# Two graph layers on one core: hand-written places for the first and last pairs, first loads through two queues, the last pair's products plain

## The chip, the cores and the metric

The kernel runs on one core of one Trainium2 chip. The metric is the device time of one execution in microseconds (us); the median of three runs is given. TensorE (PE) multiplies matrices into PSUM; its weight loads are shown as PEld. VectorE (DVE), ScalarE (ACT) and GpSimd (POOL) do the elementwise work, and SyncE (SP) and ACT issue the transfers here. Each engine works through its own list of instructions in order.

## The reference

x holds 128 graphs of 128 nodes with 512 features, float32; one 128 x 128 adjacency matrix is shared by all. Layer 0 is attention with 8 heads of 64 features, masked by the adjacency, added to x and normalised. Layer 1 is a graph attention layer whose edge scores come from two vectors, added to its input and normalised.

```python
def _L0_gnn_ref(x, adj, Wq, bq, Wk, bk, Wv, bv, Wo, bo):
    q = (x @ Wq + bq).reshape(b, n, H, HD)      # k and v alike
    scores = jnp.einsum('bqhd,bkhd->bhqk', q, k) / jnp.sqrt(jnp.float32(HD))
    scores = scores + (1.0 - adj)[None, None, :, :] * -1000000000.0
    attn = jax.nn.softmax(scores, axis=-1)
    out = jnp.einsum('bhqk,bkhd->bqhd', attn, v).reshape(b, n, d)
    return out @ Wo + bo

def _L1_gnn_ref(x, W, a, beta, mask):
    h = jnp.einsum('bnc,cf->bnf', x, W)
    s1 = jnp.einsum('bnf,f->bn', h, a1); s2 = jnp.einsum('bnf,f->bn', h, a2)
    e = jax.nn.leaky_relu(s1[:, :, None] + s2[:, None, :], negative_slope=ALPHA) * mask[None]
    att = jax.nn.softmax(e, axis=2)
    h_prime = jnp.einsum('bij,bjf->bif', att, h)
    return jax.nn.elu(h_prime + beta * h)

x = _layernorm(x + _L0_gnn_ref(x, adj, ...), axis=-1)
x = _layernorm(x + _L1_gnn_ref(x, ..., adj), axis=-1)
```

## The kernel before

**Pairs.** The 128 graphs are worked on in 64 pairs (`G = 2`, `NG = 64`); b0 and b1 are the two batches of pair g. Everything is float32.

**Products by seven.** The five matrix products of a pair (q, k, v with Wq, Wk, Wv; w with Wo; h with layer 1's W) are each split in two along the rows of the weight, along its columns and along the two batches, and made from 7 block products in place of 8 (a Strassen-Winograd scheme). The weight's sums and differences are made once (`weight_sums`, L183 to L192; one of the four operations, L189, overwrites a block of the weight itself), those of x, of the attention output oT and of the aggregated zT for each pair on POOL (`block_sum`, L222). `product(name, g, n)` issues block product n (8 matmuls of 128 columns in the trace's count for q and k, L265, 4 of 256 columns for v, w and h, L259) and accumulates in PSUM; `take_part`, `take_block` and `add_block` read the intermediate sums out, on ACT (L275, L279) and DVE (L289, L311, L319). Between two products that add into the same place a part must have been read.

**A pair's way.** `fetch_blocks` loads x in blocks of 32 and `turn_x` (L202) transposes them on DVE. q and k products, `scores` (L333), `mask` and `row_max` on DVE, `exps` and `normalise` on ACT (L355, L369). The attention weights are written to DRAM (`attn_write`, L376), read back in another arrangement (`attn_read`, L381), and turned on DVE (`turn_attn`, L398). `attend` (L408) multiplies with v, `attend_evict` (L418) gives oT, the w products add the residual x, then comes the norm: `bn_stats`, `bn_aggr`, `add_eps`, `inv_std` (a power on POOL, L441). `row_product` and `scale_s` give the edge vectors, `spread_s2` (L473) spreads one over the partitions, `edge`, `leaky`, `edge_max`, `edge_exp`, `weights` make the edge softmax for both batches, `turn_weights` (L513) and `weights_evict` transpose it, `aggregate` (L527) applies it, the h products follow, then `elu_max`, `elu_exp`, `elu_sum`, a second norm, `norm_f` (L555) and `store` (L561). The tile u that is stored has two buffers.

**Order.** Each step is put in one list by `at(place, fn, ...)`. `lay(g)` gives the steps of pair g the place `g * STEP` plus a number written by hand, the same numbers for every pair (L577 to L657). The list is sorted by place and the instructions are issued in that order (L671), so an engine's list is what the places make it. A pair's steps reach from -34.63 to 136.33 with `STEP = 37.33`: four to five pairs are under way at once.

**The start.** Before the list, SP issues the x blocks of pair 0, then wq and wk by halves of the columns in turn, wv, x of both batches, wo and w1 (L116 to L138). wq, wk and wv are loaded "turned": four transfers, each to 32 partitions (`load_turned`). ACT issues the small ones: biases, adjacency, and four broadcasts over the partitions. The two constants made from the adjacency and beta are made at once on DVE (L147, L149). `wa_column` (L158) on DVE, `wa_turn` (L168) on TensorE and `wa_centre` on DVE make the two rows of layer 1's edge vectors from w1.

**Buffers.** PSUM is one pool of eight banks for everything (`ps_mm`). The small statistics are in `st` with three buffers.

Of the kernel before, what the change touches and what calls it, by code (L numbers as in the profile page):

```python
# [22 lines left out]
def gnn_two_layers(  # L23
# [49 lines left out]
    st = ctx.enter_context(tc.tile_pool(name="st", bufs=3))  # L73
# [3 lines left out]

    def load_blocks(g):
        t = grp.tile([P, G, 4, P], F32, tag="xb", name=f"xblk_{g}", bufs=1)
        for a in range(4):  # L80
            nc.sync.dma_start(
                out=t[a * Q : (a + 1) * Q].rearrange("r t b d -> r (t b) d"),
                in_=x[g * G : (g + 1) * G, :, a * P : (a + 1) * P].rearrange(
                    "t (b r) d -> r (t b) d", r=Q
                ),
            )
        return t
# [10 lines left out]
    def load_turned(t, src, cols):  # L98
        for a in range(4):
            nc.sync.dma_start(  # L100
                out=t[a * Q : (a + 1) * Q, :, cols],
                in_=src[a * P : (a + 1) * P, cols].rearrange("(m c) f -> c m f", c=Q),
            )
# [12 lines left out]
    xblk = {0: load_blocks(0)}  # L116
    for half in range(2):
        cols = slice(half * HF, (half + 1) * HF)
        load_turned(wq_sb, wq, cols)
        load_turned(wk_sb, wk, cols)  # L120
        if half == 0:
            bq_c = column(bq, "bq_c")
            bk_c = column(bk, "bk_c")
    load_turned(wv_sb, wv, slice(0, D))
    adj_sb = cpool.tile([P, N], F32, tag="adj_sb", name="adj_sb")
    nc.scalar.dma_start(out=adj_sb, in_=adj)
    xn = {b: load_x(b) for b in range(G)}
    bo_b = broadcast(cpool, bo, D, "bo_b")
# [5 lines left out]
    ]  # L134
    wo_sb = cpool.tile([P, NC, D], F32, tag="wo_sb", name="wo_sb")
    nc.sync.dma_start(out=wo_sb, in_=wo.rearrange("(c p) f -> p c f", p=P))
    w1_sb = cpool.tile([P, NC, D], F32, tag="w1_sb", name="w1_sb")
    nc.sync.dma_start(out=w1_sb, in_=w1.rearrange("(c p) f -> p c f", p=P))  # L138
# [3 lines left out]
    make_identity(nc, ident)  # L142
    mhalf = cpool.tile([P, G], F32, tag="mhalf", name="mhalf")
# [3 lines left out]
    nc.vector.tensor_scalar(amask, adj_sb, 1.0, NEG, ALU.subtract, ALU.mult)  # L147

    beta_i = cpool.tile([P, P], F32, tag="beta_i", name="beta_i")  # L149
    nc.vector.tensor_scalar(beta_i, ident, beta_b, None, ALU.mult)  # L150
# [32 lines left out]
    def weight_sums(name, w_sb, eng):  # L183
        t = cpool.tile([P, 3, G, HF], F32, tag=f"s_{name}", name=f"s_{name}")
        a11, a21 = w_sb[:, :2, :HF], w_sb[:, :2, HF:]
        a12, a22 = w_sb[:, 2:, :HF], w_sb[:, 2:, HF:]
        s2, s3, s4 = t[:, 0], t[:, 1], t[:, 2]
        eng.tensor_tensor(s3, a11, a21, ALU.subtract)
        eng.tensor_tensor(a21, a21, a22, ALU.add)  # L189
        eng.tensor_tensor(s2, a21, a11, ALU.subtract)  # L190
        eng.tensor_tensor(s4, a12, s2, ALU.subtract)
        left[name] = {1: a11, 2: a12, 3: s4, 4: a22, 5: a21, 6: s2, 7: s3}  # L192
# [47 lines left out]
    def product(name, g, n):  # L240
# [15 lines left out]
        a, b = left[name][n], first_blocks(name if name in "wh" else "x", g)[n]  # L256
# [37 lines left out]
    def block(name, g, i, j):  # L294

        if name in "qk":
            return OUT[name][g][:, 2 * i : 2 * i + 2, j * N : (j + 1) * N]
        return OUT[name][g * G + j][:, i * HF : (i + 1) * HF]

    def result(name, g):  # L300
        if name in "qk":
            OUT[name][g] = grp.tile([P, NC, G * N], F32, tag=name, name=f"{name}T_{g}", bufs=1)
        else:
            for b in range(g * G, (g + 1) * G):
                OUT[name][b] = wk2.tile([P, D], F32, tag=name, name=f"{name}_{b}")
# [86 lines left out]
    attnT, po, x1, stats, mv, ve, rstd, s12 = ({} for _ in range(8))  # L392
# [42 lines left out]
    def add_eps(g, name):  # L435
        ve[name, g] = st.tile([P, G], F32, tag=f"ve{name}", name=f"ve_{name}_{g}")
        nc.vector.tensor_scalar(ve[name, g], mv[name, g][:, :, 1], EPS, None, ALU.add)  # L437

    def inv_std(g, name):
        rstd[name, g] = st.tile([P, G], F32, tag=f"rstd{name}", name=f"rstd_{name}_{g}")  # L440
        nc.gpsimd.tensor_tensor(rstd[name, g], ve.pop((name, g)), mhalf, ALU.pow)  # L441
# [10 lines left out]
    def scale_s(g):  # L452
        s = st.tile([P, G, 2], F32, tag="s12n", name=f"s12n_{g}")
        r = rstd["c", g].rearrange("p (i o) -> p i o", o=1).broadcast_to([P, G, 2])
        nc.vector.tensor_tensor(s, s12[g], r, ALU.mult)
        s12[g] = s

    def norm_c(b):
# [3 lines left out]
            x1[b], y.pop(b), mv["c", g][:, i, 0:1], rstd["c", g][:, i : i + 1],  # L462
# [6 lines left out]
    def spread_s2(g):  # L469

        pb[g] = ps_mm.tile([P, G, N], F32, tag="mm", name=f"pb_{g}")
        for i in range(G):
            nc.tensor.transpose(pb[g][:, i, :], s12[g][:, i, 1:2].broadcast_to([P, P]), ident)  # L473

    def edge(g, i):

        if i == 0:
            ev[g] = wk2.tile([P, G, N], F32, tag="ev", name=f"ev_{g}", bufs=1)
        nc.vector.scalar_tensor_tensor(
            ev[g][:, i, :], pb[g][:, i, :], s12[g][:, i, 0:1], adj_sb, ALU.add, ALU.mult  # L480
        )

    def leaky(g):
        ee[g] = wk2.tile([P, G, N], F32, tag="ee", name=f"ee_{g}", bufs=1)
        nc.vector.scalar_tensor_tensor(ee[g], ev[g], ALPHA, ev[g], ALU.mult, ALU.max)

    def edge_max(g):
        emax[g] = st.tile([P, G], F32, tag="emax", name=f"emax_{g}")
        nc.vector.tensor_reduce(emax[g], ee[g], AX.X, ALU.max, negate=True)

    def edge_exp(g):
        esum[g] = st.tile([P, G], F32, tag="esum", name=f"esum_{g}")
        for i in range(G):
            nc.scalar.activation(
                ee[g][:, i, :], ee[g][:, i, :], AF.Exp, bias=emax[g][:, i : i + 1],
                accum_out=esum[g][:, i : i + 1],
            )

    def edge_inv(g):
        einv[g] = st.tile([P, G], F32, tag="einv", name=f"einv_{g}")  # L500
        nc.vector.reciprocal(einv[g], esum.pop(g))

    def weights(g, i):
        if i == 0:
            att[g] = wk2.tile([P, G, N], F32, tag="att", name=f"att_{g}", bufs=1)
        nc.vector.scalar_tensor_tensor(
            att[g][:, i, :], ee[g][:, i, :], einv[g][:, i : i + 1], beta_i, ALU.mult, ALU.add
        )

    def turn_weights(g):  # L510
        pat[g] = ps_mm.tile([P, G, N], F32, tag="mm", name=f"pat_{g}")
        for i in range(G):
            nc.tensor.transpose(pat[g][:, i, :], att[g][:, i, :], ident)  # L513

    def weights_evict(g):
        attT[g] = wk2.tile([P, G, N], F32, tag="attT", name=f"attT_{g}", bufs=1)
        nc.scalar.copy(attT[g], pat.pop(g))  # L517
# [19 lines left out]
    def elu_exp(b):  # L537
        nc.scalar.activation(hp[b], hp[b], AF.Exp)  # L538

    def elu_max(b):  # L540
        u[b] = wk2.tile([P, D], F32, tag="uf", name=f"u_{b}")
        nc.vector.scalar_tensor_tensor(u[b], hp[b], 0.0, x1.pop(b), ALU.max, ALU.add)  # L542
# [4 lines left out]
    def shift(g):  # L547
        nmr[g] = st.tile([P, G], F32, tag="nmr", name=f"nmr_{g}")
        nc.vector.scalar_tensor_tensor(
            nmr[g], mv["f", g][:, :, 0], -1.0, rstd["f", g], ALU.mult, ALU.mult  # L550
# [16 lines left out]
    def fetch_x(b):  # L567
        if b not in xn:
            xn[b] = load_x(b)
# [7 lines left out]
    def lay(g):  # L577
        t0 = g * STEP
        b0, b1 = g * G, g * G + 1

        def put(*rows):
            for place, fn, *args in rows:
                at(t0 + place, fn, *args)

        put(
# [7 lines left out]
            (-9.82, take_part, "q", g, 6, 1, 0), (-9.42, result, "k", g),  # L593
            (-9.42, add_block, "k", g, 0, 0, 2, 1), (-9.15, product, "q", g, 7),
            (-8.93, take_part, "k", g, 6, 1, 0), (-8.00, product, "k", g, 7),
            (-7.11, product, "q", g, 5), (-6.81, fetch_x, b0), (-6.21, product, "k", g, 5),
            (-6.00, take_part, "q", g, 5, 1, 1), (-5.62, result, "q", g),
# [11 lines left out]
            (9.49, exps, b0, 3), (9.53, result, "v", g), (9.53, add_block, "v", g, 0, 0, 2, 1),  # L609
            (10.50, row_inv, b0), (10.92, normalise, b0, 0), (11.50, product, "v", g, 6),  # L610
            (11.52, normalise, b0, 1), (12.37, product, "v", g, 7),
            (12.59, take_part, "v", g, 6, 1, 0), (12.97, normalise, b0, 2),
            (13.57, normalise, b0, 3), (14.17, exps, b1, 0), (14.39, attn_write, b0),
            (14.96, exps, b1, 1), (16.45, exps, b1, 2), (16.72, product, "v", g, 5),
            (17.24, exps, b1, 3), (17.39, attn_read, b0), (18.03, take_part, "v", g, 5, 1, 1),
            (18.25, row_inv, b1), (18.67, normalise, b1, 0), (19.27, normalise, b1, 1),
            (19.52, add_block, "v", g, 1, 1, 7, 5), (20.25, normalise, b1, 2),
            (20.85, normalise, b1, 3), (21.67, attn_write, b1), (24.67, attn_read, b1),
# [86 lines left out]
```

## Time and profile before

| | us |
|---|---|
| three runs | 2444.12, 2446.80, 2444.03 |
| median | 2444.12 |
| the profiled execution: its time | 2446.15 |
| the profiled execution: its span, first to last instruction | 2444.3 |
| mean granted clock of TensorE | 0.992 |
| HBM read, written | 140.32 MB, 100.66 MB |

The profile is of one execution. Busy time says how long an engine worked, with its share of the span; a wait is put down to the event that came last before the engine went on. "Granted clock" is the share of full speed that TensorE's throttle allowed. In the time line a row gives the start, the length, the engine, the line and the operation, what it writes and reads, the count, and in brackets the idle time before it and what ended that.

### The profile page before, as it was taken

How to read it: one execution, taken by the hardware profiler on the slowest of the kernel's cores; microseconds unless marked ns; L12 is line 12 of the kernel's file. 1: busy time of each engine (PE TensorE's matmuls, PEld its weight loads, DVE VectorE, ACT ScalarE, POOL GpSimd, SP SyncE). 2: the span in 40 equal slices, each digit the busy share in tenths (PEclk: the TensorE clock that was granted, in tenths of full speed). 3: DMA queues.
4: the chain of work that ended last, by engine and by line, in shares of the span. 5: the costliest groups of instructions: out<-in, count | busy, mean ns of one | idle time of the engine just before them, and what ended most of it. 6: DMA issues, size and time to landing. Idle time of an engine off the chain costs nothing. (4 is left out here: it accounts for less than half of the span.)

```text
span 2444.3 us, 50024 instructions
## 1 busy us (share of the span) xinstructions
PE 2387.3 (98%) x17928; PEld 2210.7 (90%) x17928; DVE 1916.2 (78%) x4386; ACT 1489.5 (61%) x5313; POOL 859.8 (35%) x1043
## 2 busy tenths in 40 slices
PE   6999999999999999999999999999999999999995
PEld 5899999999999999999999999999999999999984
DVE  5687787787787877877877877877877878778775
ACT  3556656656656656666566566566566566666662
POOL 4233324324323333333333333243243233333331
PEclk9999999999999999999999999999999999999997
DMA  6234234234233243343343342342342432433421
GB/s 178 78 87 121 86 97 122 79 104 119 79 106 111 81 113 101 83 121 96 87 121 91 91 122 84 99 121 79 105 118 73 113 107 79 118 99 84 122 87 35
DMA packets 205144, 244.25 MB, mean 100 GB/s; under 512 B 20576, under 2 KB 153824, under 8 KB 204896
## 3 DMA queue, kind: packets, MB, share of 16 engines
q1 hardware_dynamic: 202592, 240.20, 34.2%
q8 instruction: 142, 2.33, 0.4%
q10 hardware_dynamic: 2304, 0.86, 0.2%
q14 instruction: 106, 0.87, 0.1%
HBM read 140.32 MB, written 100.66 MB: 99 GB/s over the span
## 5 line engine op out<-in xcount | busy, mean ns | idle before, releaser
L355 ACT ACTIVATE s<-s,nmax 128x128 f32<-128x128 f32 x1024 | 397.7, 394 | 0.0
L369 ACT ACTIVATE sb<-s,rinv 128x128 f32<-128x128 f32 x1024 | 327.0, 392 | 25.6 <-DVE rinv L362 24.6
L222 POOL TENSOR_TENSOR tw<-oT 128x256 f32<-128x256 f32 x64 | 46.4, 725 | 793.3 <-DVE oT L418 793.3
L389 POOL TENSOR_TENSOR x<-x,bo_b_in 128x512 f32<-128x512 f32 x128 | 163.8, 1291 | 386.3 <-DMA x<-in_x_dram 385.6
L279 ACT ACTIVATE part_q<-pq,bq_c 128x128 f32<-128x128 f32 x384 | 118.7, 360 | 259.8 <-PE pq L265 259.8
L355 ACT ACTIVATION_READ_ACCUMULATOR s<-s,nmax 128x1 f32 x1024 | 196.5, 192 | 0.0
L279 ACT ACTIVATE part_k<-pk,bk_c 128x128 f32<-128x128 f32 x384 | 119.9, 363 | 114.5 <-PE pk L265 60.7
L517 ACT COPY attT<-pat 128x256 f32<-128x256 f32 x64 | 23.8, 372 | 272.2 <-PE pat L513 272.2
L341 DVE SCALAR_TENSOR_TENSOR s<-psc,amask 128x512 f32<-128x512 f32 x256 | 164.3, 684 | 27.1 <-PE psc L333 27.1
L441 POOL TENSOR_TENSOR rstd_c<-ve_c,mhalf 128x2 f32<-128x2 f32 x64 | 67.9, 1061 | 327.0 <-DVE ve_c L437 327.0
L398 DVE STREAM_TRANSPOSE attnT<-ab 128x512 f32<-128x512 f32 x256 | 179.5, 702 | 1.0 <-DMA ab<-scr 0.8
L448 DVE SCALAR_TENSOR_TENSOR ya<-w,wa_row 128x512 f32<-128x512 f32 x256 | 173.9, 679 | 4.5
L349 DVE TENSOR_REDUCE nmax<-s 128x8 f32<-128x1024 f32 x128 | 156.2, 1220 | 4.4
L289 DVE TENSOR_TENSOR part_w<-pw,x 128x256 f32<-128x256 f32 x192 | 81.5, 425 | 92.2 <-PE pw L259 92.2
L265 PE MATMUL pq<-xT,wq_sb 128*128 128x128 f32 x1024 | 137.8, 278 | 14.4 <-DMA wq_sb<-in_L_gnn_Wq_dram 12.8
L265 PEld LDWEIGHTS pq<-xT,wq_sb 128*128 128x128 f32 x1024 | 131.8, 195 | 17.9 <-DVE xT L202 12.7
L265 PE MATMUL pk<-xT,wk_sb 128*128 128x128 f32 x1024 | 142.6, 283 | 0.2 <-DMA wk_sb<-in_L_gnn_Wk_dram 0.2
L362 DVE RECIPROCAL rinv<-rsum 128x8 f32<-128x8 f32 x128 | 25.4, 198 | 142.4 <-ACT s L355 142.4
L265 PEld LDWEIGHTS pk<-xT,wk_sb 128*128 128x128 f32 x1024 | 130.9, 194 | 4.3 <-issue 0.4
L333 PE MATMUL psc<-kT,qT 64*128 64x128 f32 x2048 | 131.8, 279 | 0.2 <-DVE kT L319 0.2
L527 PEld LDWEIGHTS pz<-attT,x 128*128 128x128 f32 x1024 | 125.9, 194 | 4.6 <-ACT attT L517 1.5
L408 PE MATMUL po<-attnT,v 128*64 128x128 f32 x2048 | 127.5, 278 | 2.6 <-DVE v L319 2.6
(150 smaller groups left out, 6635.4 us busy)
## 6 DMA issues: line engine op xcount, KB each, us to landing
scr<-sb SPq DMA_DIRECT2D x128, 512.0 KB, 2.7
ab<-scr SPq DMA_DIRECT2D x512, 128.0 KB, 3.1
xblk<-in_x_dram SPq DMA_DIRECT2D x256, 128.0 KB, 5.5
x<-in_x_dram SPq DMA_DIRECT2D x128, 256.0 KB, 5.0
out_dram<-u SPq DMA_DIRECT2D x128, 256.0 KB, 2.1
wq_sb<-in_L_gnn_Wq_dram SPq DMA_DIRECT2D x8, 128.0 KB, 4.7
wk_sb<-in_L_gnn_Wk_dram SPq DMA_DIRECT2D x8, 128.0 KB, 4.4
wv_sb<-in_L_gnn_Wv_dram SPq DMA_DIRECT2D x4, 256.0 KB, 6.1
```

What stands on the lines that cost most here:

```text
L265: nc.tensor.matmul(out[:, m * N : (m + 1) * N], a[:, c, m * P : (m + 1) * P], b[:, c, :], start=first and m == 0 and c == 0, stop=(c == 1) ...
L279: nc.scalar.activation(dst[:, m, :], src[:, m * N : (m + 1) * N], AF.Identity, bias=col)
L333: nc.tensor.matmul(psc[b][j][:, m, :], qT[g][feats, m, rows], kT[g][feats, m, rows], start=True, stop=True,)
L341: nc.vector.scalar_tensor_tensor(s_t[b][:, j * HP : (j + 1) * HP, :], psc[b][j], SCALE, amask.rearrange("p (o n) -> p o n", o=1).broadcast ...
L349: nc.vector.tensor_reduce(nmax[b], s_t[b], AX.X, ALU.max, negate=True)
L355: nc.scalar.activation(s_t[b][:, h, :], s_t[b][:, h, :], AF.Exp, bias=nmax[b][:, h : h + 1], accum_out=rsum[b][:, h : h + 1],)
L369: nc.scalar.mul(sb[b][:, :, h, :], s_t[b][:, h, :].rearrange("p (b c) -> p b c", c=Q), rinv[b][:, h : h + 1],)
L389: nc.gpsimd.tensor_tensor(xr[b], xr[b], bo_b, ALU.add)
L398: nc.vector.transpose(attnT[b].rearrange("p h (a r) -> p a h r", r=Q)[:, rows], ab[b].rearrange("p a (h c) -> p a h c", c=Q)[:, rows],)
L408: nc.tensor.matmul(po[b][j * HD : (j + 1) * HD, m, :], vb[b][:, h * HD : (h + 1) * HD], attnT[b][:, j * HP + m, :], start=True, stop=True,)
L448: nc.vector.scalar_tensor_tensor(z, y[b], 1.0, wa_row[j], ALU.mult, ALU.mult, accum_out=s12[g][:, i, j : j + 1])
L527: nc.tensor.matmul(pz[b][:, c, :], x1[b][:, c * P : (c + 1) * P], attT[g][:, i, :], start=True, stop=True,)
```

## The change

The steps of a pair stay as they are for the pairs in the middle. What differs:

- **Places.** `lay(g)` takes its steps from `rows(g)`, the list as it was, and for pairs 0, 1, 2, 3, 60, 61 and 62 takes each step's place from a table `other`. The last pair (63) has its own list, `last_rows`.
- **First loads.** The x blocks of pair 0 and wq go half through ACT's queue and half through SP's; wq and wk are loaded whole, in the order wq, wk, wv on SP. Biases, adjacency and broadcasts come on ACT behind its halves of x and wq. x, w1 and wo are loaded from places in the list, w1 ahead of wo.
- **Weight sums and constants.** `weight_sum` does one operation of four at a place of its own; products 1 and 2 can run on the weight as it was loaded, before the sums. The mask and the beta matrix get places too, and so does each `wa_column`.
- **Last pair.** w and h of pair 63 are plain products, one batch at a time, of 512 columns (`plain`): no seven block products, no parts, no block sums. As half of a row block of wo and w1 has been overwritten by then, their first half is loaded again, into wq and wk (`load_again`). `elu_exp` and `elu_max` read PSUM there. Norm, edge softmax, turn and aggregation run for each batch by itself (the functions take a batch `i` or `one`).
- **TensorE while it waits.** `keep_busy` issues matmuls on the identity into a PSUM tile that nobody reads: 20 at the start, 6 in the last pair.
- **Buffers.** `st` has six. The tiles of w, v and h are taken batch by batch when first written (`whole`), those of ev, ee, att and attT through `pair_rows`.

TensorE's order for pair 0 is now: 20 matmuls on the identity, q1, q2, q7, v1, v2, q6, k1, v7, k7, k6, q5, k2, k5, q4, q3, k3, k4, q1 of pair 1, scores of b0 (a letter and the number of its block product). Before it was q1, k1, q2, k2, q6, k6, q7, k7, q5, k5, q3, k3, q4, k4, scores, v1, v2.

The diff, cut:

```diff
-    st = ctx.enter_context(tc.tile_pool(name="st", bufs=3))
+    st = ctx.enter_context(tc.tile_pool(name="st", bufs=6))
+    def queue(a, two):
+        return nc.scalar if two and a >= 2 else nc.sync
     def load_blocks(g):
...
-            nc.sync.dma_start(
+            queue(a, g == 0).dma_start(
...
-    xblk = {0: load_blocks(0)}
-    for half in range(2):
-        cols = slice(half * HF, (half + 1) * HF)
-        load_turned(wq_sb, wq, cols)
-        load_turned(wk_sb, wk, cols)
-        if half == 0:
-            bq_c = column(bq, "bq_c")
-            bk_c = column(bk, "bk_c")
-    load_turned(wv_sb, wv, slice(0, D))
+    xblk, xn = {0: load_blocks(0)}, {}
+    load_turned(wq_sb, wq, two=True)
+    load_turned(wk_sb, wk)
+    load_turned(wv_sb, wv)
+    bq_c = column(bq, "bq_c")
+    bk_c = column(bk, "bk_c")
...
+    def load_again(t, src):
+        nc.sync.dma_start(
+            out=t[:, :2, :], in_=src[: 2 * P].rearrange("(c p) f -> p c f", p=P)
+        )
...
+    def keep_busy(n, name):
+        t = ps_mm.tile([P, P], F32, tag="mm", name=name)
+        for _ in range(n):
+            nc.tensor.matmul(t, ident, ident, start=True, stop=True)
+    keep_busy(20, "early")
...
+        if n in (1, 2) and name not in left:
+            a = W_SB[name][:, 2 * (n - 1) : 2 * n, :HF]
+        else:
+            a = left[name][n]
...
+    def plain(name, b):
+        pl[name, b] = ps_mm.tile([P, D], F32, tag="mm", name=f"pl{name}_{b}")
+        src, again = (oT, wq_sb) if name == "w" else (zT, wk_sb)
+        for c in range(NC):
+            nc.tensor.matmul(
+                pl[name, b], src[b][:, c, :], (again if c < 2 else W_SB[name])[:, c, :],
+                start=(c == 0), stop=(c == NC - 1),
+            )
+    def plain_take(b):
+        nc.vector.tensor_tensor(whole("w", b), pl["w", b], xr[b], ALU.add)
...
     def elu_exp(b):
-        nc.scalar.activation(hp[b], hp[b], AF.Exp)
+        nc.scalar.activation(whole("h", b), pl.get(("h", b), hp.get(b)), AF.Exp)
...
+    def lay(g):
+        own = last_rows(g) if g == NG - 1 else rows(g)
+        places = other.get(g, [r[0] for r in own])
+        for place, (_, fn, *args) in zip(places, own):
+            at(g * STEP + place, fn, *args)
...
+    at(19.105, load_weight, w1_sb, w1)
...
+    at(21.705, load_weight, wo_sb, wo)
...
+    at((NG - 1) * STEP + -1.779, load_again, wq_sb, wo)
+    at((NG - 1) * STEP + 0.021, load_again, wk_sb, w1)
```

## The prediction

> **What bounds the kernel now.** I read the busy table first, then busy time in chosen stretches, then the time line of both ends.
>
> ```profile
> PE 2387.3 (98%) x17928; PEld 2210.7 (90%) x17928; DVE 1916.2 (78%) x4386; ACT 1489.5 (61%) x5313; POOL 859.8 (35%) x1043
> ...
> 0.00:12.70 12.70, 0.00 (x0) 0.00 (x0) 1.82 (x4) 1.28 (x1) 1.43 (x8) 1.00 0.81 178
> 12.70:35.40 22.70, 20.27 (x152) 18.50 (x152) 10.60 (x18) 5.00 (x16) 12.77 (x13) 1.00 0.94 239
> 35.40:54.00 18.60, 11.30 (x50) 9.41 (x51) 16.98 (x34) 12.96 (x55) 12.25 (x10) 0.77 0.24 86
> 54.00:80.00 26.00, 24.21 (x195) 22.26 (x194) 13.53 (x25) 12.02 (x48) 7.73 (x10) 0.97 0.29 75
> ...
> 2200.00:2237.00 37.00, 37.00 (x282) 34.42 (x282) 29.37 (x69) 23.23 (x83) 13.11 (x16) 1.00 0.35 102
> 2344.00:2381.00 37.00, 36.74 (x275) 33.78 (x274) 29.53 (x67) 23.11 (x83) 10.55 (x12) 1.00 0.25 81
> 2381.00:2394.00 13.00, 6.43 (x46) 4.72 (x45) 12.34 (x32) 3.20 (x9) 1.06 (x1) 0.87 0.32 102
> 2394.00:2412.00 18.00, 14.14 (x72) 12.35 (x72) 11.03 (x32) 4.43 (x9) 7.44 (x10) 0.96 0.08 29
> 2412.00:2432.00 20.00, 12.84 (x48) 9.89 (x48) 9.04 (x23) 6.56 (x15) 3.54 (x5) 0.69 0.04 14
> 2432.00:2444.30 12.30, 0.00 (x0) 0.00 (x0) 4.79 (x11) 2.78 (x4) 0.69 (x1) 0.61 0.17 64
> ```
>
> After the time, a row gives the length, then busy us of PE, weight loads, DVE, ACT and POOL, the granted clock, the DMA share and GB/s. The middle has no slack on TensorE: 37.00 of 37.00 us at clock 1.00, and scores of pair 1 (67.64) and of pair 63 (2360.79) stand 62 pairs and 2293.2 us apart, 36.99 us a pair. Everything else is lost at the ends: before 12.7, in 35.4 to 54, and after 2381.
>
> ```profile
> 22.00:24.00 2.00, 1.86 (x16) 1.87 (x17) 1.20 (x3) 0.14 (x1) 0.00 (x0) 1.00 1.06 249
> 26.00:28.00 2.00, 1.72 (x15) 1.53 (x15) 1.18 (x3) 1.25 (x4) 1.92 (x2) 1.00 1.05 409
> ```
>
> ```profile
> 12.75 2.05 PE L265 MATMUL pq<-xT,wq_sb 128*128 128x128 f32 x8 [12.75 <-DMA wq_sb<-in_L_gnn_Wq_dram]
> ...
> 14.95 2.05 PE L265 MATMUL pk<-xT,wk_sb 128*128 128x128 f32 x8 [0.15 <-DMA wk_sb<-in_L_gnn_Wk_dram]
> ...
> 16.79 1.61 PE L265 MATMUL pq<-xT,wq_sb 128*128 128x128 f32 x8
> ...
> 18.24 1.06 PE L265 MATMUL pk<-xT,wk_sb 128*128 128x128 f32 x8
> ...
> 24.36 1.28 POOL L188 TENSOR_TENSOR s_v<-wv_sb 128x512 f32<-128x512 f32 x1 [9.46 <-DMA wv_sb<-in_L_gnn_Wv_dram]
> ...
> 33.37 1.99 PE L259 MATMUL pv<-wv_sb,xT 128*128 128x256 f32 x8
> ```
>
> Three things are to be seen. The turned weights arrive at 249 GB/s and the plain ones behind them at 409, with the DMA engines full both times. TensorE's first products run at half speed (2.05 against 1.06 us). And wv is there only at 24.4.
>
> ```profile
> 2390.67 2.83 PE L408 MATMUL po<-attnT,v 128*64 128x128 f32 x24 [2.64 <-DVE v L319]
> ...
> 2430.56 1.03 PE L259 MATMUL eh<-w_sb,th 128*128 128x256 f32 x4
> ...
> 2432.40 0.69 DVE L542 SCALAR_TENSOR_TENSOR u<-h,x 128x512 f32<-128x512 f32 x1 [0.35 <-DMA out_dram<-u]
> ...
> 2439.79 1.52 ACT L555 ACTIVATE u<-u,nmr,rstd_f 128x512 f32<-128x512 f32 x2 [4.39 <-DVE nmr L549]
> ```
>
> After TensorE's last product (2431.6) another 12.7 us of elementwise work and stores follow; its start waits for a store, since u has two buffers.
>
> **The sum.** The profiled execution took 2446.15 us: a span of 2444.3 and 1.85 around it. It lies 2.0 above the median of 2444.12. The middle is bound by TensorE, whose list of instructions is the same before and after from pair 5 to pair 60, so I set it at nothing; what hides DVE's and ACT's changes there is TensorE's full 37 of 37 us (DVE has 7.6 us free per pair). Each end is costed as time lost to TensorE: elapsed time less products at full speed. From the time line's steady part, a q or k product costs 0.89 us (2351.08 to 2351.97), a v, w or h product 0.865, both batches' scores 2.06, attend 1.97, both aggregates 1.95.
>
> *Start, before.* Up to the first product of pair 2 (80.20) TensorE does 28 q/k products (25.0), 17 v/w products (14.7), two pairs of scores (4.1), attend (2.0) and eight column turns (0.9): 46.7. Lost: 80.2 - 46.7 = 33.5 us.
>
> *Start, after.* x and wq now go half through ACT's queue and ahead of the columns and broadcasts. They are 0.52 + 1.05 MB; with traffic from about 2 us and 240 GB/s they land at 8.6 (at 409 GB/s at 5.9, as before at 12.7). I take the first product at 9. DVE's two turns (1.30) and POOL's block sums (0.72 each) fit before or beside it. The 20 early matmuls on the identity (40 records, first at 0.26 us, then 0.11) fill about 7 us of a TensorE that has nothing else, cost nothing there, and take the 2.5 us of half speed away that the four quoted product rows show (2.05 + 2.05 + 1.61 - 3 x 1.06). But TensorE's new order is q1, q2, q7, then v1 and v2, and only then q6 and all of k, and the SP queue still carries wk ahead of wv. So TensorE stands at v1 from 9 + 2.7 = 11.7 until wv is there, with 11 q/k products behind it and everything that needs them. Ahead of and with wv go x 0.52, wq, wk, wv 3 x 1.05 and ACT's broadcasts and adjacency 0.85 MB: 4.52 MB. At 240 GB/s from 2 us that is 20.8; at 409 it is 13.0; as before it is 24.4. The nearest row is the turned weights' own 249, with some help from two queues on different partitions: I take 20. The stall is then 8.3 us, and the clock is lost again: 2.5 us as above (0 if the wait is short).
>
> After v1 fifteen products stand ready, so scores of pair 0 start at about 20 + 13.3 + 2.5 = 36, later than the 30.92 of before, but with v1, v2, v7 and pair 1's q1 done. From there the order interleaves pair 1's products with pair 0's softmax and round trip through DRAM. The 7.3 idle us of 35.4 to 54 (the column turns that waited for DVE, v7 behind DVE's masks) mostly go: DVE's list to attend (two masks and maxima 5, eight columns 5.7, two centrings 4, adds and turns 3.5: 18 us) is as long as TensorE's (two scores, 19 products: 20 us). I leave 3.5 us for waits (1.8 is idle in 54 to 80 now; 8 at worst, as in 35.4 to 54). w1 and wo are issued behind x, still before DVE's first column. Lost: 20 - 2.7 + 2.5 + 3.5 = 23.3. Gain at the start 33.5 - 23.3 = 10 us; with wv at 13.0 and no stall 21, with wv at 24.4 and 8 us of waits 1.
>
> The row on queues: both stretches above show the engines full (1.06, 1.05). The Trainium skill (Trainium Kernel Development and Optimization, Key Constraints) says that DMAs from different queues share the same 16 engines, so that a second queue saves issue time only; by it wv would land at 20.8 and the gain would be 9. The same skill (TensorE: Matmul & The Clock Gate, Part 1) puts a fall to half clock after an idle window of about 3.4 us and as long to recover, by which the stall would undo what the early matmuls bought and cost 1.7 instead of 2.5.
>
> *End, before.* From scores of pair 63 (2360.79) to the end 83.5 us; work in it 42 products (36.3), scores 2.06, attend 1.97, three pairs of aggregates 5.85, five small turns 2.1: 48.3. Lost: 35.2.
>
> *End, after.* The last pair's w and h become plain, by batch: four products of eight 512-column records, 0.43 each by the 256-column pitch of 0.216, 13.8 us for 12.1; 1.7 dearer, but no block sums on POOL, no parts, no order among them. The first half of wo and w1 is fetched again into wq and wk (0.5 MB each) once TensorE is past the last q and k; only the attention write 11 us later stands behind it on SP. The chain of batch 127, from scores of 126: mask, max and evictions on DVE to 7.2; on ACT 126's exponentials and two copies to 8.3, two of 127's and 126's eight normalisations 11.6, two norm_f 13.2, six exponentials, four copies and eight normalisations 19.5; write, read and landing 7 (2372.73 to 2375.44, 1.75 of issue, median 3.1), two turns 1.4: 28; attend, evict, plain w, take 5.8 and hand-overs 1: 35. Statistics, power, scale with 126's row products between: 40. Spread, edge, leaky, max, exp, inverse, weights, turn, evict 3, with ten hand-overs and DVE's other work 3: 46. Aggregate and evict 2: 48; both plain h 6.9: 55. Then 11: elu_max of 126 still waits for pair 62's store (exp 0.65, norm_f 0.82, issue 0.45, landing 2.1), eleven DVE operations 5, power, shift, norm_f and store 4. Sum 66. Two additions: 3 us of slips, and 2.5 of half clock, as TensorE waits most between 39 and 48 (the six late matmuls cover 1.3; 2412 to 2432 shows 0.69 now). 71.5, against 83.5, and the order has done 1 us more work by then: gain 13 (18.5 without additions, 5.5 if as much again slips).
>
> Sum: 2446.15 - 10 - 13 = 2423.15 for a profiled execution, 2421 for the median.
>
> **Rivals.** *wv in time:* the two queues reach 409 GB/s as the plain loads do. Then there is no stall, the start gains 18 to 21: 2411. For it: 409 was reached. Against: only with 128 partitions written, not 32.
>
> *The end gains little:* in-order ACT or DVE puts the last pair's softmax behind pair 62's work and the round trip ends last; 5 instead of 13 at the end, 5 at the start: 2434. For it: DVE is busy 12.34 of 13 us in 2381 to 2394.
>
> *Slower, a new wait in the middle:* w, v and h tiles are now taken one batch at a time at their first use, and st has six buffers; if that puts a wait on an add which a product follows, it is paid in each of 57 pairs. TensorE waits there now for qT seven times, 2.0 us in all, so that hand-over is tight. It decides from 28/57 = 0.5 us a pair; at 0.55 the time is 2452. Against: the order of instructions is the same and DVE has 7.6 us free.
>
> *The matmuls on the identity do not hold the clock:* 2.5 us more at either end, 2426, inside the forecast.
>
> **How the numbers follow.** Forecast 0.64 (2412 to 2430, the last rival in it), wv in time 0.15, little at the end 0.14, slower 0.07. The range from 2408 to 2434 holds the forecast, most of the second and half of the third. A measurement tells 0.2%, 4.9 us, from no change: faster 0.64 + 0.15 + 0.10 = 0.89, same 0.04 (the third's upper end), slower 0.07.
>
> **What would show it.** In the changed kernel's trace: early matmuls from 1.5 to about 9 us; the first pq at 9; an idle PE before pv, released by the DMA of wv, at about 20; scores of pair 0 at 36 and no wait over 2 us until pair 2; 36.99 us a pair; 71 us from the last pair's scores to the end. A pv that follows pq without a gap, or another period, makes the prediction wrong.

## The result and the profile after

| | before | after |
|---|---|---|
| runs beside each other, median (lowest to highest), us | 2445.2 (2444.03 to 2446.8) | 2425.53 (2423.86 to 2426.46) |
| ratio, 95% interval | | 0.9918 (0.9901 to 0.9936) |
| span of the profiled execution, us | 2444.3 | 2424.1 |
| scores of pair 0 start at, us | 30.92 | 41.48 |
| scores of pair 2 | 99.84 | 93.02 |
| scores of pair 5 | 210.82 | 205.37 |
| scores of pair 7 | 284.78 | 283.57 |
| scores of pair 61 | 2286.30 | 2283.44 |
| scores of pair 63 | 2360.79 | 2359.70 |
| from there to the end, us | 83.5 | 64.4 |

The forecast was 2421, the range 2408 to 2434. The time fits; its two halves do not. The forecast gave 10 us to the start and 13 to the end. The scores of the last pair stand only 1.1 us earlier than before, and 19.1 of the 20.2 us by which the span is shorter come after them. The table shows the rest: the start is 5.5 us ahead at pair 5, 1.2 at pair 7.

First the busy times of the changed kernel's page, to be held against the same line of before: 2.4 us more busy time on TensorE in a span 20 us shorter. The matmuls on the identity, 7.1 us at the start and 1.5 in the last pair, are in it.

```profile
PE 2389.7 (99%) x17956; PEld 2205.0 (91%) x17956; DVE 1912.0 (79%) x4385; ACT 1488.4 (61%) x5310; POOL 854.8 (35%) x1037
```

Then its busy time in chosen stretches, with the columns of the rows of before: length, busy us of PE, weight loads, DVE, ACT and POOL, the granted clock, DMA share, GB/s.

```profile
8.00:16.00 8.00, 3.38 (x29) 3.03 (x27) 3.52 (x7) 1.91 (x3) 1.39 (x2) 1.00 0.72 137
...
35.40:54.00 18.60, 18.60 (x160) 17.63 (x159) 13.98 (x28) 11.63 (x47) 10.19 (x9) 1.00 0.18 45
54.00:80.00 26.00, 25.32 (x202) 22.21 (x201) 21.50 (x44) 18.48 (x78) 12.86 (x14) 1.00 0.26 87
...
200.00:248.00 48.00, 44.81 (x369) 40.78 (x369) 36.45 (x81) 26.21 (x93) 13.45 (x16) 1.00 0.26 78
2311.00:2348.00 37.00, 35.54 (x262) 31.56 (x262) 30.76 (x71) 22.70 (x81) 16.34 (x19) 1.00 0.28 94
...
2380.00:2400.00 20.00, 19.17 (x102) 12.73 (x101) 17.89 (x45) 5.81 (x15) 5.32 (x7) 1.00 0.17 53
2400.00:2416.00 16.00, 13.94 (x60) 8.54 (x59) 11.10 (x30) 7.82 (x18) 0.70 (x1) 1.00 0.17 66
2416.00:2424.10 8.10, 0.00 (x0) 0.00 (x0) 3.29 (x10) 1.88 (x3) 1.10 (x2) 0.72 0.17 65
```

and the kernel before in two of these stretches:

```profile
200.00:248.00 48.00, 48.00 (x388) 44.93 (x388) 39.36 (x91) 28.63 (x100) 15.66 (x18) 1.00 0.37 100
...
2311.00:2348.00 37.00, 37.00 (x283) 34.42 (x282) 30.75 (x69) 23.34 (x83) 13.28 (x16) 1.00 0.34 99
```

Four things are to be seen. From 35.4 to 54 TensorE is now full (11.30 of 18.60 before). From 8 to 16 the DMA engines are not: 137 GB/s at a share of 0.72, with wk and wv still to come. Two places are new losses: 3.2 us between 200 and 248, where before had 48.00 of 48.00, and 1.5 in 2311 to 2348, where it had 37.00 of 37.00. And the end is tight: 19.17 of 20 and 13.94 of 16 at clock 1.00, where the rows of before had 6.43 of 13 and 14.14 of 18.

The time line of the start (pq, pk and pv are the PSUM tiles of q's, k's and v's products, psc of the scores):

```profile
1.36 7.11 PE L155 MATMUL early<-ident 128*128 128x128 f32 x40 [1.36 <-POOL ident masks.py:199]
10.43 2.02 PE L299 MATMUL pq<-xT,wq_sb 128*128 128x128 f32 x16 [1.96 <-DMA wq_sb<-in_L_gnn_Wq_dram]
...
25.66 3.75 PE L293 MATMUL pv<-wv_sb,xT 128*128 128x256 f32 x8 [12.32 <-DMA wv_sb<-in_L_gnn_Wv_dram]
29.20 1.57 PE L299 MATMUL pq<-tx,s_q 128*128 128x128 f32 x8
...
41.48 0.71 PE L385 MATMUL psc<-kT,qT 64*128 64x128 f32 x8
...
3.44 9.86 SPq L104 DMA_DIRECT2D wk_sb<-in_L_gnn_Wk_dram  x4
13.34 3.18 SPq L104 DMA_DIRECT2D wv_sb<-in_L_gnn_Wv_dram  x4
```

and what SP waited for in the first 26 us:

```profile
SPq L104 <- DMA wq_sb<-in_L_gnn_Wq_dram: 5.4, 1, 5.4
SPq L104 <- DMA bk_c<-in_L_gnn_bk_dram: 3.0, 1, 3.0
```

The mechanism is the forecast's: TensorE does q1, q2, q7 and then stands at v1 for wv, 12.3 us, and comes back at half clock (3.75 us for eight records instead of 1.89). Its size is not: wv is there at 25.7, no earlier than in the kernel before (24.4). The last two rows of the time line show where the time went. SP issues wk from 3.44 to 13.30 and wv only from 13.34 on; in between it waits for transfers that were issued earlier to land, wq and a bias column.

### The profile page after: what moved, and what is told of

Its sections match the earlier page's. It is cut to its first block, busy times and chain, and to the rows that moved or that the text cites. A ratio compares the mean times of both kernels' runs of the same rounds, so it can differ in the third digit from the quotient of the medians.

```text
span 2424.1 us, 50042 instructions
## 1 busy us (share of the span) xinstructions
PE 2389.7 (99%) x17956; PEld 2205.0 (91%) x17956; DVE 1912.0 (79%) x4385; ACT 1488.4 (61%) x5310; POOL 854.8 (35%) x1037
## 4 chain that ended last, share of the span: by engine, by line
PE 92%; DVE 3%; DMA 2%; ACT 1%; SPq 1%; issue 1%; POOL 0%; ACTq 0%; DVEq 0%; POOLq 0%
PE pw L293 11%; PE pk L299 11%; PE pv L293 11%; PE ph L293 11%; PE pq L299 11%; PE eq L299 9%; PE psc L385 5%; PE po L460 5%; PE pz L595 5%; PE ev L293 4%; PE ew L293 4%; PE eh L293 4%; PE pat L582 1%; DMA xblk<-in_x_dram 1%; PE pb L539 1%
## 5 line engine op out<-in xcount | busy, mean ns | idle before, releaser
L585 ACT COPY attT<-pat 128x256 f32<-128x256 f32 (+1 forms) x65 | 24.0, 369 | 268.1 <-PE pat L582 268.1
L293 PE MATMUL pv<-wv_sb,xT 128*128 128x256 f32 x512 | 123.6, 384 | 12.3 <-DMA wv_sb<-in_L_gnn_Wv_dram 12.3
L309 ACT COPY part_v<-pv 128x256 f32<-128x256 f32 x192 | 69.9, 364 | 104.1 <-PE pv L293 104.0
L385 PEld LDWEIGHTS psc<-kT,qT 64*128 64x128 f32 x2048 | 119.5, 188 | 11.8 <-issue 11.3
```

The source lines that it names most:

```text
L293: nc.tensor.matmul(out, b[:, c, :], a[:, c, :], start=first and c == 0, stop=(c == 1), skip_group_check=True,)
L385: nc.tensor.matmul(psc[b][j][:, m, :], qT[g][feats, m, rows], kT[g][feats, m, rows], start=True, stop=True,)
```

## The experiments

Twelve kernels were run, each beside the kernel before, whose median lay between 2445.9 and 2446.2; a1 was run ten times, the others four. The intervals reach about 4 us to each side and those of neighbouring kernels overlap, so a difference of 4 us between two of them rests on the places in their traces as well as on the medians. "Ahead" is how much earlier than in the kernel before a pair's scores start in the profiled execution; "end" runs from the scores of pair 63 to the end.

| run | median us | ratio, 95% interval | pair 0's scores at | ahead at pair 5 | pair 7 | pair 63 | end |
|---|---|---|---|---|---|---|---|
| the changed kernel | 2425.5 | 0.9918 (0.9901 to 0.9936) | 41.48 | 5.5 | 1.2 | 1.1 | 64.4 |
| a1 start only | 2443.3 | 0.9987 (0.9978 to 0.9996) | 40.16 | 5.6 | 1.3 | 0.9 | 82.7 |
| a2 small loads late | 2421.3 | 0.9893 (0.9878 to 0.9908) | 36.20 | 10.6 | 7.4 | 6.8 | 64.5 |
| a3 pair 3 common | 2421.5 | 0.9899 (0.9883 to 0.9916) | 39.90 | 6.4 | 6.4 | 7.0 | 64.1 |
| a4 k first | 2422.1 | 0.9898 (0.9883 to 0.9913) | 36.85 | 10.0 | 5.0 | 3.7 | 64.5 |
| b1 columns late | 2424.1 | 0.9913 (0.9896 to 0.9930) | 38.72 | 8.8 | 4.5 | 3.3 | 64.2 |
| b2 broadcasts late | 2420.0 | 0.9895 (0.9880 to 0.9910) | 34.94 | 11.5 | 4.9 | 6.9 | 64.2 |
| b3 no late identity | 2427.7 | 0.9920 (0.9905 to 0.9935) | 40.67 | 5.1 | 0.7 | -1.1 | 64.1 |
| b4 no early identity | 2426.9 | 0.9922 (0.9907 to 0.9937) | 39.74 | 6.7 | 0.2 | -2.7 | 64.5 |
| c1 b2 and a3 | 2417.4 | 0.9885 (0.9870 to 0.9900) | 35.23 | 11.2 | 10.7 | 12.1 | 64.1 |
| c2 c1, k first, masks later | 2416.1 | 0.9881 (0.9866 to 0.9895) | 36.19 | 10.7 | 10.7 | 11.5 | 64.4 |
| c3 c1, wv first, masks later | 2413.3 | 0.9869 (0.9853 to 0.9886) | 33.18 | 14.0 | 13.7 | 12.6 | 64.0 |
| c4 last pair common | 2454.6 | 1.0041 (1.0026 to 1.0056) | 39.38 | 7.0 | 3.7 | 0.3 | 91.7 |

From pair 7 to pair 63 the profiled executions drift by up to 3.4 us against each other, so the start is read at pairs 5 and 7. The six kernels with the first loads of the changed one and its order of TensorE at the start have pv between 24.2 and 25.7, five of them below 24.5; the changed kernel's own execution is the latest of them.

**a1: which half carries the gain.**

```diff
-        own = last_rows(g) if g == NG - 1 else rows(g)
-        places = other.get(g, [r[0] for r in own])
+        own = rows(g)
+        places = other.get(g if g < NG - 4 else None, [r[0] for r in own])
-    at((NG - 1) * STEP + -1.779, load_again, wq_sb, wo)
-    at((NG - 1) * STEP + 0.021, load_again, wk_sb, w1)
```

> The changed kernel with the end's part undone: the last pair is laid by rows() like the others, pairs 60 to 62 keep the common places, wo and w1 are not fetched again. Theory S (the forecast's split, start 10 us, end 13): about 2435, and scores of pair 61 some 10 us earlier than before. Theory E (the changed kernel's trace: scores of pairs 62 and 63 stand only 1.1 us earlier than before, so nearly all of the 20 us comes from the end): 2441 to 2444, pair 61's scores 1 to 3 us earlier than before, and the end from pair 63's scores 83.5 as before.

Theory E holds: 2443.3, the end 82.7 us. The whole start part is worth 2.7 us of the time (1 to 5 by the interval), not 10; the end part is worth the other 17.8.

**a2, b1, b2: what makes wv late.** In a2 all small loads are issued by SP behind wv; in b1 only the three columns, in b2 only the rest.

```diff
 def broadcast(pool, src, n, name):
-        nc.scalar.dma_start(out=t, in_=src.rearrange("(o n) -> o n", o=1).broadcast_to([P, n]))
+        nc.sync.dma_start(out=t, in_=src.rearrange("(o n) -> o n", o=1).broadcast_to([P, n]))
 def column(src, name):
-        nc.scalar.dma_start(out=t, in_=src.rearrange("(c p) -> p c", p=P))
+        nc.sync.dma_start(out=t, in_=src.rearrange("(c p) -> p c", p=P))
-    nc.scalar.dma_start(out=adj_sb, in_=adj)
+    nc.sync.dma_start(out=adj_sb, in_=adj)
```

> The changed kernel with the bias columns, adj, beta, a1 and bo issued by SP behind wv instead of by ACT beside wk. Theory I (issue: the 512 pieces of 4 bytes of each column hold up SP's descriptors, so that wv's loads are issued only from 13.3 us and the DMA engines run at 0.62 to 0.79 from 8 to 16): wv's last load is issued by about 8 us and wv lands at 16 to 18 (3.7 MB at 240 to 250 GB/s from 1.5 us), the wait for wv falls from 12.3 to 4 to 6 us, and scores of pair 0 stand at about 34 instead of 41.5. Theory B (the turned loads are slow whatever stands beside them): wv within 1 us of 25.7, nothing else changed. What reaches the time is less than what the scores gain, by theory E of the run before: 0 to 5 us.

> The changed kernel with only the three bias columns (512 pieces of 4 bytes each, 2 KB) issued by SP behind wv; adj, beta, a1 and bo (0.85 MB) stay with ACT beside wk. Theory C (the pieces of 4 bytes hold the engines and SP's issue): wk and wv issued by about 11 us as in the run with all small loads late, pv at 20 to 22, scores of pair 0 at 36 to 38. Theory V (the volume of the broadcasts, 3.5 us at 240 GB/s, is what stands ahead of wv): pv at 24 to 26, scores at 40 to 41.5.

> The mirror image: adj, beta, a1 and bo behind wv on SP, the three columns stay with ACT beside wk. Theory C: pv still at 23 to 26, scores at 40 to 41.5. Theory V: pv at 20 to 22, scores at 36 to 38. If both matter, each of the two runs gains part of the 5.3 us.

In a2 the scores come 5.3 us earlier, and the busy row of its stretch 8 to 16 shows the engines full where the changed kernel had 0.72:

```profile
8.00:16.00 8.00, 4.36 (x24) 4.10 (x24) 2.77 (x4) 0.00 (x0) 1.31 (x2) 0.79 1.07 227
```

The wait for wv fell to 5.1 us (pv at 20.02), but wv came 2 us later than the 16 to 18 expected, and SP issued its last load at 10.64 and not by 8. Theory B, that the turned loads are slow whatever stands beside them, falls. These are pv in a2 and in b1:

```profile
20.02 3.75 PE L293 MATMUL pv<-wv_sb,xT 128*128 128x256 f32 x8 [5.13 <-DMA beta_b_in<-in_L_gnn_beta_dram]
...
22.36 3.75 PE L293 MATMUL pv<-wv_sb,xT 128*128 128x256 f32 x8 [9.99 <-DMA xblk<-in_x_dram]
```

The profile puts both waits down to another transfer, but the last load of wv landed just before pv, at 19.88 and 22.23. Of the two parts, b1 puts pv at 22.36 and b2 at 19.94, against 24.2 to 25.7: the 0.85 MB of broadcasts and adjacency count for most, 4 to 6 us, the columns of 2 KB each for 2 to 3. The two do not add, as a2, which has both, is no earlier than b2. Either edit alone fills the engines from 8 to 16 (a share of 1.07 at 256 GB/s in b1, 1.10 at 200 in b2). So theory C, which I held, is at best the smaller half; V is nearer. Issue is not free either way: in b2 SP still takes from 3.66 to 9.64 us for wk's four transfers. Why its next issue waits for an earlier one to land I didn't settle.

b2's time lines of TensorE and DVE show what comes next:

```profile
19.94 3.40 PE L293 MATMUL pv<-wv_sb,xT 128*128 128x256 f32 x8 [7.46 <-DMA wv_sb<-in_L_gnn_Wv_dram]
...
20.26 1.01 DVE L170 TENSOR_SCALAR beta_i<-ident,beta_b_in 128x128 f32<-128x128 f32 x1 [6.34 <-DMA beta_b_in<-in_L_gnn_beta_dram]
...
21.32 1.75 DVE L215 TENSOR_TENSOR s_k<-wk_sb 128x512 f32<-128x512 f32 x1
```

DVE stands in order at beta's scaling for 6.3 us, with wk's block sums behind it.

**a3: the 4 us that vanish between pairs 5 and 7.** This is what TensorE waited for in the changed kernel from 200 to 248 us:

```profile
PE ph L293 <- ACT part_h L309: 1.7, 1, 1.7
PE pq L299 <- DVE qT L371: 1.3, 1, 1.3
```

Up to place 89 pair 3's own list is the common one. From there it puts h products 6, 5, 3 and 4 3.4 to 6.8 later and the steps that follow them up to 8.7 earlier; these are the places from 201 to 245.

```diff
-        places = other.get(g, [r[0] for r in own])
+        places = other.get(g if g != 3 else None, [r[0] for r in own])
```

> The changed kernel with pair 3 at the common places instead of its own list. Theory P (pair 3's later places for its last products put waits on TensorE between 205 and 246 us, and 4 of the start's 5.5 us go there): scores of pair 6 stand 5 us ahead of before instead of 1.5, and pair 62's about 4 to 5 us ahead, time 3 to 4 us shorter than the changed kernel. Theory W (the start's gain is used up by buffers and by DVE and ACT, which are a pair behind, wherever pair 3's pieces stand): pair 6 again within 1 us of where the changed kernel has it, time the same.

```profile
200.00:248.00 48.00, 48.00 (x395) 44.53 (x394) 39.74 (x85) 28.31 (x103) 13.16 (x16) 1.00 0.25 78
```

Theory P holds. All waits there are gone, pair 7 is 6.4 us ahead and the time is 4.0 us shorter. The whole table agrees: the nine kernels with pair 3's own list lose 3.3 to 6.6 us between pairs 5 and 7, the four without it 0 to 0.5. The two that lose most, b2 and b4 (6.6 and 6.5), are those whose granted clock also fell to half in this stretch (0.96 on average over 200 to 248, against 1.00 in the changed kernel).

**a4: waiting for the earlier weight.** Places of v1, v2, v7 and what takes them, in pair 0's list:

```diff
-  14.09 (v1), 14.96 (v2), 17.62 (v7), 16.05 (take_part v1), 19.785 (add_block v)
+  22.30 (v1), 22.35 (v2), 22.37 (v7), 22.40 (take_part v1), 23.50 (add_block v)
```

> The changed kernel with pair 0's v products 1, 2 and 7 moved behind its first six k and q products, so that TensorE waits for wk (landed about 21 us) and not for wv (25.7). If the wait for wv is what sets pair 0's scores: they stand 3 to 4 us earlier (37.5 to 38.5), wv is there when v1's turn comes, and the granted clock is still 0.5 after the wait. If DVE's block sums of wk or the biases set it: less than 1.5 us. In the time no more than 2 us, if theory E holds.

The scores move to 36.85, 4.6 us earlier and slightly beyond the expectation; k1 starts at 21.37 at half clock:

```profile
21.37 2.04 PE L299 MATMUL pk<-xT,wk_sb 128*128 128x128 f32 x8 [6.16 <-DMA wk_sb<-in_L_gnn_Wk_dram]
```

Against the other kernels with these loads (39.4 to 40.7) the scores are 2.5 to 3.8 us earlier. By the medians 3.4 us reach the time, more than the 2 I allowed: the start's gain isn't swallowed in general. What swallows most of it is pair 3's list, which takes 5.0 us between pairs 5 and 7 here too.

**b3 and b4: the matmuls on the identity.** Each run leaves one `keep_busy` line out.

> The changed kernel without the six matmuls on the identity in the last pair (no part of the computation). The forecast's step (TensorE waits most between 39 and 48 us after the last pair's scores, the six cover 1.3, and what isn't covered costs up to 2.5 us of half clock): clock below 1.00 between 2402 and 2414 and 1 to 2.5 us longer. Rival (pair 62's h products, moved to this place, keep TensorE busy enough): clock stays 1.00 up to the last product, time within 0.5 us of the changed kernel's.

> The changed kernel without the twenty matmuls on the identity at the start (no part of the computation). Theory N (TensorE stands at v1 for 10 to 12 us anyway and falls to half clock there with or without them): q1, q2 and q7 run at half clock (2.05 us for eight records instead of 1.06) but within the wait, pv and pair 0's scores stand where they stood, time the same within 1 us. Rival (the clock is then half for longer behind the wait): scores 1 to 2.5 us later.

Without the late six the clock stays at full speed, by b3's row of the stretch 2402 to 2414:

```profile
2402.00:2414.00 12.00, 9.56 (x40) 6.03 (x41) 9.72 (x28) 6.16 (x15) 0.70 (x1) 1.00 0.12 44
```

and the end takes 64.1 us instead of 64.4. They do nothing there. The median is 2.1 us above the changed kernel's, but not by the six, which come after the last pair's scores: these stand 2.2 us later in b3, and the end is no longer. Without the early twenty the first products do run at half clock, by b4's time line,

```profile
10.29 3.76 PE L298 MATMUL pq<-xT,wq_sb 128*128 128x128 f32 x16 [10.29 <-DMA bv_c<-in_L_gnn_bv_dram]
```

but within the wait for wv: the scores stand at 39.74, inside the 39.4 to 41.5 of the runs with the twenty. They buy 1.7 us where nobody waits for it. (The ratios of b3 and b4, 0.9920 and 0.9922, lie inside the changed kernel's interval.)

**c4: what the end's gain hangs on.** The first line of a1's diff alone, and the second fetch left out: pairs 60 to 62 keep their own lists.

> The changed kernel with the last pair alone as before the change: seven products for w and h by pair, softmax and normalisation for both batches together, no second fetch of wo and w1; pairs 60 to 62 keep their own lists. Theory O (the last pair's own order by batch and plain products give the end's 18 us, by the shorter chain of batch 127 and a tail of 8.5 instead of 12.7): 2438 to 2444. Theory L (the pieces of pairs 60 to 62 that were moved into the last pair's waits give it): 2425 to 2432.

It is slower than the kernel before (1.0041, 1.0026 to 1.0056), 91.7 us from the last scores to the end, and outside both expectations. Theory L falls, and theory O was too mild. c4's waits of TensorE from 2300 on:

```profile
PE pat L582 <- DVE att L573: 6.4, 2, 3.3
PE pb L539 <- DVE s12n L516: 5.4, 2, 5.1
PE ph L293 <- ACT part_h L309: 3.5, 5, 2.2
```

The edge softmax by pair and the parts of the h products are what the last pair's own order by batch and its plain products take away; how much is due to the order and how much to the plain products no run separates. The lists of pairs 60 to 62 alone cost 9.0 us of the end and 11.3 of the time against a1, which has the common lists there (82.7 and 2443.3): they put pair 62's work into a last pair that isn't laid out for it. The reverse, common lists for 60 to 62 with the last pair's own, wasn't tried.

**c1, c2, c3: put together.** c1 is b2 and a3. c2 and c3 also have

```diff
-    at(16.605, make_beta)
-    at(16.895, make_mask)
+    at(19.140, make_beta)
+    at(19.150, make_mask)
...
+        if b == G * (NG - 1):
+            u[b] = wk2.tile([P, D], F32, tag="u", name=f"u_{b}", bufs=1)
```

which puts beta's scaling and the mask behind wk's sums on DVE and gives batch 126 a third u. c2 also has a4's places, c3 instead

```diff
-    load_turned(wk_sb, wk)
-    load_turned(wv_sb, wv)
+    load_turned(wv_sb, wv)
+    load_turned(wk_sb, wk)
```

> The changed kernel with the broadcasts and adj behind wv and pair 3 at the common places: two edits that gained 5.5 and 4.0 us alone. If they cost in different places (the wait for wv before 25.7; TensorE's waits for pair 3's late pieces between 205 and 246 us) the gains add: scores of pair 6 some 11.5 us ahead of before, 2415 to 2417. If the earlier start only runs into the same work that holds pair 6 back, 2419 to 2421.

> The run before, and in it pair 0's v products behind its first six k and q products, beta's scaling and the mask behind wk's four block sums on DVE (in the run with the broadcasts late DVE stood 6.3 us at beta's scaling with wk there), and u of batch 126 in a buffer of its own, so that its first write doesn't wait for a store. TensorE then waits for wk, at about 17 us, instead of for wv at 20: scores of pair 0 at 31 to 33 instead of 35, the half clock still paid; the third u takes the wait of 3.0 us away but the chain goes over batch 127, so at most 0.7 at the end. 2411 to 2414; if DVE's sums of wk (0.7 each, 1.7 beside POOL's) set the order instead, no more than 1 us below the run before.

> The run before the last one, with wv's loads ahead of wk's and TensorE's order as the changed kernel has it, the masks behind wk's sums and the third u. If the bytes ahead of a weight set its landing: wv at 14 to 16, pv waits 2 to 4 us instead of 7.5 to 12.3, then q6, then a second wait for wk to about 20, scores of pair 0 at 30 to 32, 2410 to 2414. If the landing isn't set by the order of issue, pv at 20 as before and the time that of the first run.

In c1 the two gains add (11.1 ahead at pair 6; the median, 2417.4, is just above the 2415 to 2417 expected). c2 missed its 2411 to 2414: TensorE was early with k1 (15.85) but then stood 4.0 us at q4, because DVE waited in its order for pair 1's x before it added q, and came back at half clock (time lines of DVE and TensorE):

```profile
26.91 1.31 DVE L232 STREAM_TRANSPOSE xT<-xblk 128x512 f32<-128x512 f32 x2 [4.56 <-DMA xblk<-in_x_dram]
...
28.58 2.07 PE L299 MATMUL eq<-tx,wq_sb 128*128 128x128 f32 x8 [3.96 <-DVE qT L371]
```

c3 does better, and is faster than both kernels: 2413.28 (2412.72 to 2414.03). By its time line the waits at the start are down to 3.1 and 0.6 us, with the scores 1 to 3 us later than expected, as wk came at 21.0 and not 20, and 0.9 us is lost behind the same turn of pair 1's x:

```profile
15.99 3.01 PE L293 MATMUL pv<-wv_sb,xT 128*128 128x256 f32 x8 [3.07 <-DMA wv_sb<-in_L_gnn_Wv_dram]
...
33.18 1.16 PE L385 MATMUL psc<-kT,qT 64*128 64x128 f32 x16
```

The third u changed nothing: the end is 64.0 to 64.4 in c1, which lacks it, c2 and c3.

## Why the prediction was right in the sum and wrong in its parts

**The wait for wv (the term "I take 20").** Right in place, wrong in size: 25.7 in place of 20, and 24.2 to 24.5 in the five other kernels with the same loads, so about at its worst bound of 24.4 or beyond it. The forecast divided 4.52 MB by 240 GB/s and so took the engines as full from 2 us on. They moved 137 GB/s between 8 and 16, while SP's issue stood still. The 249 GB/s it leaned on belong to the stretch just before the plain loads of x landed (24.6 and 25.3); in 18 to 20 and 20 to 22 the kernel before had 219 and 225. And then it took a value below its own quotient for "some help from two queues", which no row showed. b2 and c3 show that what is queued ahead decides: 4 to 6 us for 0.85 MB and 4 more for the order of two weights (pv at 19.94 and 15.99). This term alone is -5.7 us in the profiled execution, -4.2 to -4.5 in the five.

**The half clock behind it (2.5).** Right: 3.75 instead of 1.89 and 1.57 instead of 1.06, 2.4 in all, and not the 1.7 of the forecast's other estimate, as the clock was back only 4.6 us after pv's start; and so was it that the stall undoes what the early matmuls buy (b4).

**The waits after the scores (3.5).** Too dear: 0 in 35.4 to 54, 0.7 in 54 to 80, so +2.8. With these two terms the forecast's 10 becomes 7.1; the trace has 6.8 at pair 2. The first product, at 10.43 and not 9, costs nothing, as TensorE would only stand at v1 sooner.

**The middle ("I set it at nothing").** This step failed. The period is unchanged (37.04 us from pair 10 to pair 60, 37.07 before). But the forecast had TensorE's list as "the same before and after from pair 5 to pair 60", and it isn't: pair 3's changed places lie at 201 to 245 us, and TensorE's order differs between the scores of pairs 5 and 6. There the price was 4.3 us (a3). Two stretches stood in no term at all: from pair 2 to pair 5, where the lead fell from 6.8 to 5.5 us, and from pair 60 to the scores of pair 63, where 1.5 us were lost in 2311 to 2348, among the moved pieces of pairs 60 to 62. So 6.8 us of gain came down to 1.1.

**The end (71.5 us).** Mis-sized by 7.1. The chain of batch 127 to its last product, 55 by sum, took 55.9 (2415.6), and not by chance: its marks on the way lay 1 to 2 us late (both turns done at 29.9 for 28, the first plain h at 48.8 for 48). The two additions, 5.5 us, were hardly paid: 0.9 of slips, and the clock stayed at 1.00. The six matmuls are not what held it (b3). That pair 62's h products, moved into these waits, did so is likely but not shown: c4 has them moved too and had 0.91 on average between 2400 and 2420, so the last pair's own list seems to have a part in it. And the 11 us behind the last product, whose listed terms add up to 13.0, were 8.5:

```profile
2413.74 1.88 PE L351 MATMUL plh<-w_sb,zT 128*128 128x512 f32 x4
...
2414.33 0.69 DVE L610 SCALAR_TENSOR_TENSOR u<-plh,x 128x512 f32<-128x512 f32 x1 [3.00 <-DMA out_dram<-u]
...
2415.71 0.60 ACT L606 ACTIVATE h<-plh 128x512 f32<-128x512 f32 x1 [2.14 <-PE plh L351]
```

These rows of the changed kernel's time line show why: batch 126's wait for a store, which the forecast put on the chain, ends at 2414.3, while batch 127's product still runs. c2 and c3 take the wait away and gain nothing. The low bound of the end's gain was also added up wrong: "as much again" as the 5.5 us of additions off 13 leaves 7.5, not 5.5.

**The rivals.** "wv in time" fell (25.7). "The end gains little" fell. The slower one, a new wait in each pair, fell by the period; a small relative of it, in single pairs, was there. "The matmuls on the identity do not hold the clock" was true of the start, where the wait undoes them, and idle at the end, where they weren't needed; neither had a price.

By the traces the forecast had too much ahead of the last pair by 9 us (10 against 1.1) and too little at the end by 6 (13 against 19.1); by a1's time, by 7 and 5 (2.7 and 17.8). That the total is right is luck: two errors of opposite sign met.

## What to carry to other kernels

When one pair's places are moved, follow its pieces to the last one, not to the end of the stage that was meant: pair 3's later h products cost 4 us where pairs 5 and 6 begin. Here 0.85 MB ahead of the first weights cost 4 to 6 us of a weight's landing and the order of two weights another 4: the weight that TensorE needs next should stand first, with constants behind it and, on the engine that uses them, behind the sums that gate products. A total that fits proves no split; one run with half of the change undone (a1) does.

## What the runs showed of the hardware

**A gap of 2.3 us was enough for half clock.** With the early matmuls the gap before the first product was 1.1 to 2.4 us in ten runs, whose sixteen records then took 2.02 us. In a3 (2.30) and a2 (2.76) they took 2.44 and 2.66: the granted clock fell to 0.50 at 11.3 and 11.7, more than a microsecond after the products had begun again, and was back at 1.00 some 3.4 us later, when TensorE had just become idle. The Trainium skill (TensorE: Matmul & The Clock Gate, Part 1) puts the fall behind an idle window of about 3.4 us that runs freely. The length of the slow stretch agrees, and so does the free running: in each of the fourteen traces the granted clock changes only at whole multiples of 3.41 us from one another. But the window need not be idle. These are the windows behind which the clock fell in a3 and a2, and the one in a1, with a gap of 2.44, behind which it didn't:

```profile
7.87:11.28 3.41, 1.43 (x13) 1.46 (x14) 1.43 (x3) 0.00 (x0) 1.48 (x3) 1.00 0.83 121
...
8.31:11.72 3.41, 1.20 (x11) 1.23 (x12) 1.22 (x2) 0.00 (x0) 1.00 (x2) 1.00 1.08 222
...
8.55:11.96 3.41, 1.64 (x15) 1.67 (x16) 1.64 (x3) 0.15 (x1) 0.86 (x2) 1.00 0.65 117
```

TensorE was busy 42 and 35% of the first two and 48% of the third. Of all forty falls in the traces none followed a window that was busy more than 44%, and at full clock no window that was busy less than 41% went without one. So where a gap lies in the window decides, and a gap well below a window can be enough. Behind the wait for wv the same grid made the half clock last 2.9 us (b2) to 5.4 (b3).

**Turned loads.** While turned weights were almost all that was under way, the engines were full at 227 GB/s (a2's row of 8 to 16) and at 219 and 225 (the kernel before in 18 to 20 and 20 to 22). The changed kernel's 254 at 16 to 18 is no such figure: about half of the engines' time went to the broadcasts there. The Trainium skill (SBUF — State Buffer, Door 1: The DMA port swizzle) gives about 218 GB/s as the limit of a transfer to partitions 0 to 31 and 436 for all 128; here four transfers to different blocks of 32 partitions lay at the first or slightly above it.

**DVE beside POOL.** A block sum of wk takes DVE 0.69 us alone, and 1.66 to 1.75 in b2, where POOL makes wv's sums at the same time, POOL's own going from 1.26 to 1.61. In c3, where wv's sums come first, DVE's are 0.69 again except the one that overlaps (0.84).
